# Layer 0's heads: one load for the products of four heads, and a new order of the first loads in SyncE's queue

## The chip, the core and the metric

The kernel runs on one core of a Trainium2 chip. A core has five engines, each with its own instruction stream: TensorE (PE in the profile; PEld is its weight loads), VectorE (DVE), ScalarE (ACT), GpSimd (POOL) and SyncE (SP), which only issues transfers. SyncE, ScalarE and GpSimd can each issue DMAs; the profile lists the queues as q1 (SyncE), q10 (ScalarE) and q0 (GpSimd). All of them are served by the core's 16 DMA engines. The metric is device time in microseconds (us), the median of several runs.

## The reference

Four graph layers run one after the other on x (4096 nodes, 256 features) with one adjacency matrix, each with a residual and a layernorm. The change is in layer 0, an attention layer with 8 heads of 32 channels:

```python
node_feats = (x @ W.T + b).reshape(num_nodes, num_heads, half)
logit_parent = (node_feats * a[None, :, :half]).sum(axis=-1)
logit_child = (node_feats * a[None, :, half:]).sum(axis=-1)
attn_logits = logit_parent[:, None, :] + logit_child[None, :, :]
attn_logits = jax.nn.leaky_relu(attn_logits, 0.2)
attn_logits = jnp.where(jnp.abs(adj_matrix)[..., None] != 0.0, attn_logits, 0.0)
attn_probs = jax.nn.softmax(attn_logits, axis=1)
out = jnp.einsum('ijh,jhc->ihc', attn_probs, node_feats)
...
x = _layernorm(x + _L0_gnn_ref(x, ..., adj), axis=-1)
x = _layernorm(x + _L1_gnn_ref(x, adj, L1_gnn_weight, L1_gnn_bias), axis=-1)
```

The exponential of leaky_relu(p + c) is a product of a factor of the row and a factor of the column, with one pair of factors where p + c is positive and another where it is not. So the softmax's sums split into products that don't depend on the sign, and a correction over the edges where the sign is positive.

## The kernel before, in words

**Layer 0 has two stages.** `sums0` reads x and the adjacency, computes the features, and multiplies the adjacency with the features times the factors for all heads at once. It leaves in DRAM: `nad` (the adjacency as bytes), `gmd` (the column factors times the features, in three bfloat16 parts, 396 bytes for one row and head), `lpd` (the parent logits, one row of 4096 numbers a head) and `zd` (the products that don't depend on the sign, 33 numbers a row and head). A branch follows (`choose0`, line 375): all engines read one number that says whether the factors stay in range, and otherwise run another version, `general0`.

**Then come the heads**, the loop that the change touches (lines 296 to 364). It runs over two halves of four heads, within a half over four chunks of 1024 rows (`it`), within a chunk over the half's four heads (`hh`). One pass of the inner loop, a head, goes over 32 blocks of 128 columns in 8 groups of 4 (`g`). For each group

- four comparisons of the row logits `lpb` (one row broadcast to 128 partitions, 0.52 MB) with a column's logit make `sg`: on VectorE (line 270) in groups 2, 5 and 7, on ScalarE (line 276) in the others;
- VectorE combines `sg` with the adjacency's bytes `na` into the mask `gt` (line 272 or 278);
- TensorE multiplies 32 times (line 331): the mask's 128x128 pieces with `gm`, 198 columns wide, into `acc`.

After the last group VectorE reduces `acc` (line 337), scales it (341), adds the halves (344) and `z` (345), and divides by the last column (347, 348). There are four slots for `gt`, three for `sg`, two each for `lpb` and `z`. The masks of groups 0 and 1 of the first head are made in advance, in `sums0` (`early_mask`), with their factors in `gm0` and the first head's row logits in `first`; so the first head asks for groups 2 to 7 first.

**The loads of the heads** stand in three queues. SyncE issues, for the first chunk of a half, `na` (line 301) and `gm` of the first head (303) group by group, then `gm` of the other three heads (306), and for the second half x and the rows kept of the first half (308, 310). GpSimd issues `lpb` (line 236) and `z` (316) head by head, and the store of a chunk's result (354). The next layers' weights are loaded by `add_w1` (lines 778 to 784): layer 1's weight and bias on ScalarE's queue (through `load_w`, line 115, and `load_row`, 121), three attention weights of layer 2 on GpSimd's. The call stands at the end of layer 0's code, but the tiles are free earlier, and the scheduler puts these loads near the start of the heads.

**The order of the work** in the heads is set by the framework's scheduler, from the order of the code, the free slots and what an instruction depends on; the loops of `sums0` and of layers 1 to 3 are ordered by hand. [...]

Layer 1 begins with TensorE's transposes of X (line 370) and the product with `weight1` (line 823).

Of the kernel before, what the change touches and what calls it, by code (L numbers as in the profile page):

```python
# [9 lines left out]
F32 = mybir.dt.float32  # L10
# [13 lines left out]
P = 128  # L24
# [26 lines left out]
def row_broadcast(v, n):  # L51

    return bass.AP(tensor=v.tensor, offset=v.offset, ap=[[0, P], [1, n]])


class Net:
# [159 lines left out]
    def layer0(self):  # L216
        nc, tc, NB, D, N = self.nc, self.tc, self.NB, self.D, self.N
        H, C = 8, 32
        C1 = C + 1
        IT = min(1024, N)  # L220
        Q = IT // P
        keep = self.ctx.enter_context(tc.tile_pool(name="l0k", bufs=1, space=DRAM))
        self.fits = keep.tile([1, 1], I32, name="fits")
        with ExitStack() as ctx:
            pool = ctx.enter_context(tc.tile_pool(name="l0", bufs=1))
# [6 lines left out]
            fac = pool.tile([P, 4, NB, H], F32, name="fac")  # L232
            lpd = dram.tile([H, N], F32, name="lpd")

            def row_logits(t, h, it):
                nc.gpsimd.dma_start(t, bass.AP(tensor=lpd.tensor, offset=lpd.offset + h * N + it * IT, ap=[[0, P], [1, IT]]))
                return t

            first = pool.tile([P, IT], F32, name="lpb0")
# [5 lines left out]
            zd = dram.tile([NB, P, H, C1], F32, name="zd")  # L245
# [19 lines left out]
            def mask(gt, sg, na, lpb, g, h):  # L265

                bits = [t.rearrange("p k i -> p (k i)").bitcast(U32) for t in (gt, sg, na)]
                if g % 8 in (2, 5, 7):
                    for k in range(4):
                        nc.vector.tensor_scalar(sg[:, k, :], lpb, nlc[:, 4 * g + k, h:h + 1], 2.0 ** -5,  # L270
                                                op0=ALU.is_ge, op1=ALU.mult, saturate=False)
                    nc.vector.tensor_tensor(*bits, ALU.bitwise_and)
                else:

                    for k in range(4):
                        nc.scalar.activation(sg[:, k, :], lpb, AF.Sign, scale=-1.0, bias=nlc[:, 4 * g + k, h:h + 1],  # L276
                                             saturate=False)
                    nc.vector.scalar_tensor_tensor(bits[0], bits[1], SIGN_ABOVE, bits[2],  # L278
                                                   op0=ALU.logical_shift_right, op1=ALU.bitwise_and)

            self.sums0(both, nlc, fac, lpd, nad, zd, gmd, lambda: row_logits(first, 0, 0), early_mask)
            self.choose0(fac, zd, gmd, gm0)

# [4 lines left out]
            work = ctx.enter_context(tc.tile_pool(name="l0w", bufs=2))  # L288
# [2 lines left out]
            gm = gp.tile([P, NB, H // 2, 6 * C1], BF16, name="gm")  # L291
            na = gp.tile([P, NB, IT], U8, name="na")

            later = []
            per_head = Q // 2 // (H // 2)
            for half in range(2):
                for it in range(N // IT):
                    i0 = it * Q
                    begun = 2 if it == half == 0 else 0
                    for g in [*range(begun, NB // K), *range(begun)]:  # L300
                        nc.sync.dma_start(na[:, g * K:(g + 1) * K], nad[it, :, g * K:(g + 1) * K, :])
                        if it == 0:
                            nc.sync.dma_start(gm[:, g * K:(g + 1) * K, 0], gmd[half, :, g * K:(g + 1) * K, 0])
                    for hh in range(1, H // 2 if it == 0 else 0):
                        for g in range(0, NB // K, 2):
                            nc.sync.dma_start(gm[:, g * K:(g + 2) * K, hh], gmd[half, :, g * K:(g + 2) * K, hh])
                    if half:
                        nc.sync.dma_start(X[:, i0:i0 + Q, :], xr[:, i0:i0 + Q, :])
                        y0 = work.tile([P, Q, D // 2], F32, name="y0", bufs=1)
                        nc.sync.dma_start(y0, yd[i0:i0 + Q].rearrange("b p d -> p b d"))  # L310
                    y = work.tile([P, Q, H // 2, C], F32, name="y")
                    for hh in range(H // 2):
                        h = half * (H // 2) + hh
                        lpb = row_logits(work.tile([P, IT], F32, name="lpb"), h, it) if h or it else first
                        z = work.tile([P, Q, C1], F32, name="z")
                        nc.gpsimd.dma_start(z, zd[i0:i0 + Q, :, h].rearrange("b p c -> p b c"))
                        acc = psum.tile([P, Q, 256], F32, name="acc")
                        for g in range(NB // K):

                            head0 = g < 2 and half == it == hh == 0  # L320
                            if head0:
                                gt = gt0[:, g * K:(g + 1) * K, :]
                            else:
                                gt = work.tile([P, K, IT], FP8, name="gt", bufs=4)
                                sg = work.tile([P, K, IT], FP8, name="sg", bufs=3)
                                mask(gt, sg, na[:, g * K:(g + 1) * K, :], lpb, g, h)
                            for k in range(K):
                                jc = g * K + k
                                for q in range(Q):

                                    nc.tensor.matmul(acc[:, q, :6 * C1], gt[:, k, q * P:(q + 1) * P],  # L331
                                                     gm0[:, jc, :] if head0 else gm[:, jc, hh, :],
                                                     start=(jc == 0 and q % 2 == 0),
                                                     stop=(jc == NB - 1 and q % 2 == 1))

                        red = work.tile([P, Q, 2 * C1], F32, name="red")
                        nc.vector.tensor_reduce(red, acc[:, :, :6 * C1].rearrange("p q (s c) -> p q c s", s=3),
                                                AX.X, ALU.add)

                        red = red.rearrange("p q (s c) -> p q s c", s=2)  # L340
                        nc.vector.tensor_mul(red, red, fac[:, 0:2, i0:i0 + Q, h].rearrange("p s q -> p q s").unsqueeze(3)
                                             .to_broadcast([P, Q, 2, C1]))
                        t1 = red[:, :, 0, :]
                        nc.vector.tensor_add(t1, t1, red[:, :, 1, :])
                        nc.vector.tensor_add(t1, t1, z)
                        r = work.tile([P, Q], F32, name="r")
                        nc.vector.reciprocal(r, t1[:, :, C])
                        nc.vector.tensor_mul(y[:, :, hh, :], t1[:, :, :C], r.unsqueeze(2).to_broadcast([P, Q, C]))
                        for xs in later[:per_head]:
                            self.layernorm(work, xs, xs, nc.gpsimd, bufs=6)  # L350
                        del later[:per_head]
                    y = y.rearrange("p q h c -> p q (h c)")
                    if not half:
                        nc.gpsimd.dma_start(yd[i0:i0 + Q].rearrange("b p d -> p b d"), y)
                        continue

                    if i0 + Q == NB:
                        self.add_w1()
                    engine = nc.vector if i0 + Q == NB else nc.gpsimd
                    for q in range(0, Q, 2):  # L360
                        xs = X[:, i0 + q:i0 + q + 2, :]
                        nc.gpsimd.tensor_add(xs[:, :, :D // 2], xs[:, :, :D // 2], y0[:, q:q + 2])
                        engine.tensor_add(xs[:, :, D // 2:], xs[:, :, D // 2:], y[:, q:q + 2])
                        later.append(xs)
            self.later = later
            acc = psum.tile([P, Q, 256], F32, name="acc").rearrange("p q c -> p (q c)")
            for c in range(2):
                half = acc[:, c * 512:(c + 1) * 512]
# [408 lines left out]

    def add_w1(self):
        nc, pool = self.nc, self.pool1
        self.weight1, self.bias1 = self.load_w(pool, self.w1, "w1"), self.load_row(pool, self.b1, "bias1")  # L780
        aw1, aw3, aw2, _ = self.attention_parts()
        for t, w in ((aw1, self.aw1t), (aw3, self.aw3t)):
            nc.gpsimd.dma_start(t, w.rearrange("(c p) m -> p c m", p=P))
        nc.gpsimd.dma_start(aw2, self.aw2t)

    def attention_parts(self):

# [1250 lines left out]
```

## Time and profile before

| | |
|---|---|
| median of 3 runs | 3946.61 us (3946.18 to 3950.18) |
| the profiled execution | 3947.67 us, its span 3946.0 us |
| mean granted TensorE clock | 0.994 |
| line 331 on TensorE | 577.3 to 1284.8 us |
| TensorE, VectorE, ScalarE busy from 577 to 1285 us | 701.35, 685.73, 663.92 of 708 us |
| loads of lpb; of z (32 each, GpSimd's queue) | 512 KB, 4.1 us to landing; 132 KB, 3.3 us |
| issue of one z; of one lpb on GpSimd | 0.90 us; 0.56 us |

All times are counted from the span's start. A group of instructions is shown with its line, engine, operation, the tiles that it writes and reads, how often it ran, its busy time, the mean of one, and the idle time of its engine just before it with what ended most of that. "to landing" is the time from a DMA's issue until its data is there. A wait is put down to what ended last, by inference from the semaphores. The granted clock (PEclk) is a share of TensorE's full speed.

### The profile page before, as it was taken

To read this page: it belongs to the slowest core of one execution; us is meant where nothing else is said; L and a number is where in the kernel's file an instruction comes from. 1 tells how busy PE (TensorE), PEld (TensorE's weight loads), DVE (VectorE), ACT (ScalarE), POOL (GpSimd) and SP (SyncE) were. 2 spreads that over 40 slices of the span, in tenths; PEclk is the share of its full clock that TensorE was granted. 3 is DMA by queue.
4 is the path that set the end of the run, shared out by engine and by line. 5 is a ranking of instruction groups with operands and counts; after the bars stand their busy time and mean duration, and the time that the engine had idled before them with its cause. 6 is when DMAs were issued, how large, how long until landed. Compare 5 with 4: busy or idle time off the path is not lost. (4 is left out here: it accounts for less than half of the span.)

```text
span 3946.0 us, 68781 instructions
## 1 busy us (share of the span) xinstructions
PE 3879.5 (98%) x25081; PEld 3361.6 (85%) x25081; DVE 2993.1 (76%) x6637; ACT 2742.9 (70%) x5121; POOL 1167.5 (30%) x1402
## 2 busy tenths in 40 slices
PE   8999999999999999999999999999999999999898
PEld 7999999999999887578888888866888888888686
DVE  6444449999999444667878788838999999999364
ACT  5434449999998322578888888736888888888232
POOL 1222220111444222311111111114665565555211
PEclk9999999999999999999999999999999999999999
DMA  4666667244221796533332323463333333335541
GB/s 118 204 207 203 219 196 209 82 117 120 77 92 44 281 374 254 148 113 98 98 99 93 103 94 103 156 195 102 102 107 117 105 106 105 117 107 195 199 145 45
DMA packets 317565, 557.38 MB, mean 141 GB/s; under 512 B 72806, under 2 KB 139894, under 8 KB 313110
## 3 DMA queue, kind: packets, MB, share of 16 engines
q1 hardware_dynamic: 242528, 396.99, 30.9%
q0 software_dynamic: 32224, 98.75, 7.7%
q10 hardware_dynamic: 42454, 57.04, 4.2%
q8 instruction: 203, 3.33, 0.3%
q14 instruction: 156, 1.28, 0.1%
HBM read 386.71 MB, written 165.94 MB: 140 GB/s over the span
## 5 line engine op out<-in xcount | busy, mean ns | idle before, releaser
L1411 PE MATMUL ps_a<-X,aT 128*128 128x256 f32 x4096 | 968.9, 379 | 1.3 <-ACT h L1555 1.1
L1411 PEld LDWEIGHTS ps_a<-X,aT 128*128 128x128 f32 x4096 | 773.4, 190 | 127.5 <-issue 3.9
L331 PE MATMUL acc<-gm,gt 128*128 128x198 bf16 x8192 | 701.4, 248 | 11.7 <-DVEq L375 5.3
L331 PEld LDWEIGHTS <-gt 128*128 128x128 fp8e4 x8192 | 699.5, 97 | 13.5 <-issue 7.2
L276 ACT ACTIVATE sg<-lpb,nlc 128x1024 fp8e4<-128x1024 f32 x632 | 663.9, 1135 | 43.4 <-DVE gt L278 29.3
L180 PE MATMUL ps_r<-XD,adj_piece 128*128 128x512 f32 x1888 | 528.4, 414 | 0.0
L601 PE MATMUL pz<-src,ar 128*128 128x264 f32 x4096 | 500.0, 284 | 0.4 <-DVE big L399 0.4
L601 PEld LDWEIGHTS pz<-src,ar 128*128 128x128 f32 x4096 | 499.8, 188 | 0.5 <-issue 0.5
L1138 ACT ACTIVATE ja<-e,nc 128x2048 uint8<-128x2048 f32 x240 | 480.9, 2004 | 2.0
L1404 ACT COPY aT<-ps_tp 128x512 f32<-128x512 f32 x512 | 296.4, 579 | 216.0 <-PE ps_tp L1402 208.7
L180 PEld LDWEIGHTS ps_r<-XD,adj_piece 128*128 128x128 f32 x1888 | 332.9, 189 | 68.8 <-issue 12.9
L1203 DVE MAX8 cand<-v 128x8 f32<-128x256 f32 x1024 | 347.2, 412 | 4.4
L1253 DVE SCALAR_TENSOR_TENSOR e<-e,edge 128x512 f32<-128x512 f32 x512 | 347.6, 750 | 2.1
L561 ACT ACTIVATE nb<-ar 128x512 uint8<-128x512 f32 x256 | 147.6, 623 | 279.5 <-DVE ar L558 170.8
L1402 PE MATMUL ps_tp<-ident,e 128*128 128x128 f32 x2048 | 308.0, 273 | 0.7 <-DVE e L1253 0.7
L1199 DVE SCALAR_TENSOR_TENSOR v<-e,hi 128x2048 f32<-128x2048 f32 x128 | 300.3, 2346 | 2.4
L1402 PEld LDWEIGHTS ps_tp<-ident,e 128*128 128x128 f32 x2048 | 256.8, 142 | 52.1 <-DVE e L1253 0.9
L558 DVE CAST ar<-a 128x1024 fp32r<-128x1024 f32 x128 | 88.9, 694 | 266.7 <-PE pz L601 266.6
L270 DVE TENSOR_SCALAR sg<-lpb,nlc 128x1024 fp8e4<-128x1024 f32 x384 | 285.8, 779 | 6.0 <-SPq L375 3.9
L1047 ACT ACTIVATE e<-ps_logit 128x1024 f32<-128x1024 f32 x256 | 260.2, 1027 | 26.5 <-PE ps_logit L1045 26.3
L1045 PE MATMUL ps_logit<-kT,q 128*128 128x512 f32 x1024 | 274.2, 409 | 1.4 <-ACT e L1047 1.2
L854 PE MATMUL ps_adj<-XD,adj_piece 128*128 128x512 f32 x1024 | 239.8, 394 | 0.0
(404 smaller groups left out, 5599.0 us busy)
## 6 DMA issues: line engine op xcount, KB each, us to landing
adj_piece<-adjs SPq DMA_DIRECT2D x552, 256.0 KB, 2.7
a<-in_adjt_dram SPq DMA_DIRECT2D x256, 256.0 KB, 3.1
adjs<-adj_piece SPq DMA_DIRECT2D x96, 512.0 KB, 3.1
na<-nad SPq DMA_DIRECT2D x64, 512.0 KB, 5.5
lpb<-lpd POOLq DMA_DIRECT2D x32, 512.0 KB, 4.1
nad<-nb POOLq DMA_DIRECT2D x128, 128.0 KB, 2.7
na<-nad ACTq DMA_DIRECT2D x16, 1024.0 KB, 8.8
gmd<-gb POOLq DMA_DIRECT2D x64, 198.0 KB, 2.8
```

Of the source, the lines that this page charges most:

```text
L180: nc.tensor.matmul(ps, a[:, k, :], rhs(jc).rearrange("p s d -> p (s d)"), start=(jc == 0), stop=(jc == self.NB - 1))
L270: nc.vector.tensor_scalar(sg[:, k, :], lpb, nlc[:, 4 * g + k, h:h + 1], 2.0 ** -5, op0=ALU.is_ge, op1=ALU.mult, saturate=False)
L276: nc.scalar.activation(sg[:, k, :], lpb, AF.Sign, scale=-1.0, bias=nlc[:, 4 * g + k, h:h + 1], saturate=False)
L331: nc.tensor.matmul(acc[:, q, :6 * C1], gt[:, k, q * P:(q + 1) * P], gm0[:, jc, :] if head0 else gm[:, jc, hh, :], start=(jc == 0 and q % 2 ...
L601: nc.tensor.matmul(pz[q][:, t, :W], ar[:, q, k, :], src[:, jc, t, s], start=(jc == 0 and s == 0), stop=(jc == NB - 1 and s == 1))
L1138: nc.scalar.activation(ja, e[:, s * HALF:(s + 1) * HALF], f, bias=nc1, accum_out=fs[:, i + s:i + s + 1])
L1199: nc.vector.scalar_tensor_tensor(v, ec, hi, ec, op0=ALU.is_lt, op1=ALU.mult, accum_out=sb[:, s:s + 1])
L1203: nc.vector.max(cand[:, 8 * j:8 * j + 8], v[:, k * 256:(k + 1) * 256])
L1253: nc.vector.scalar_tensor_tensor(ec, ec, edge[:, j:j + 1], ec, op0=ALU.is_ge, op1=ALU.mult)
L1402: nc.tensor.transpose(pt[:, k * P:(k + 1) * P], e[:, jc * P:(jc + 1) * P], self.ident)
L1404: nc.scalar.copy(aT, pt)
L1411: nc.tensor.matmul(pa[:, :D], aT[:, k * P:(k + 1) * P], X[:, jc, :], start=(jc == 0), stop=(jc == NB - 1))
```

## The change

The products `z` of a half's four heads are read in one load for each chunk, with one slot (so each element run is 528 bytes and not 132). In the very first chunk this load and head 1's row logits are issued by SyncE, behind the loads of group 4; in the other chunks GpSimd issues z, ahead of the chunk's row logits in the code. `first` and `second` serve heads 0 and 1 of the first chunk. `add_w1` issues all five loads on SyncE's queue; as built they stand behind the four loads of x and ahead of the second chunk's bytes.

```diff
-            def row_logits(t, h, it):
-                nc.gpsimd.dma_start(t, bass.AP(...))
+            def row_logits(t, h, it, queue=nc.gpsimd):
+                queue.dma_start(t, bass.AP(...))
                 return t
...
+            def products_of(i0, half, queue):
+                z = work.tile([P, Q, H // 2, C1], F32, name="z", bufs=1)
+                queue.dma_start(z, zd[i0:i0 + Q, :, half * H // 2:(half + 1) * H // 2].rearrange("b p h c -> p b h c"))
+                return z
...
                         if it == 0:
                             nc.sync.dma_start(gm[:, g * K:(g + 1) * K, 0], gmd[half, :, g * K:(g + 1) * K, 0])
+                        if begun and g == 4:
+                            z = products_of(i0, half, nc.sync)
+                            second = row_logits(work.tile([P, IT], F32, name="lpb"), 1, 0, nc.sync)
+                    if not begun:
+                        z = products_of(i0, half, nc.gpsimd)
...
-                        lpb = row_logits(work.tile([P, IT], F32, name="lpb"), h, it) if h or it else first
-                        z = work.tile([P, Q, C1], F32, name="z")
-                        nc.gpsimd.dma_start(z, zd[i0:i0 + Q, :, h].rearrange("b p c -> p b c"))
+                        lpb = (first, second)[h] if it == 0 and h < 2 else \
+                            row_logits(work.tile([P, IT], F32, name="lpb"), h, it)
...
-                        nc.vector.tensor_add(t1, t1, z)
+                        nc.vector.tensor_add(t1, t1, z[:, :, hh, :])
...
     def add_w1(self):
         nc, pool = self.nc, self.pool1
-        self.weight1, self.bias1 = self.load_w(pool, self.w1, "w1"), self.load_row(pool, self.b1, "bias1")
+        self.weight1 = pool.tile([P, 2, self.D], F32, name="w1")
+        nc.sync.dma_start(self.weight1, self.w1.rearrange("(c p) m -> p c m", p=P))
+        self.bias1 = pool.tile([P, self.D], F32, name="bias1")
+        nc.sync.dma_start(self.bias1, row_broadcast(self.b1, self.D))
         aw1, aw3, aw2, _ = self.attention_parts()
         for t, w in ((aw1, self.aw1t), (aw3, self.aw3t)):
-            nc.gpsimd.dma_start(t, w.rearrange("(c p) m -> p c m", p=P))
-        nc.gpsimd.dma_start(aw2, self.aw2t)
+            nc.sync.dma_start(t, w.rearrange("(c p) m -> p c m", p=P))
+        nc.sync.dma_start(aw2, self.aw2t)
```

More of the change, by code (lines that the diff above doesn't have):

```diff
@@ L233, in layer0 @@
             lpd = dram.tile([H, N], F32, name="lpd")
-            def row_logits(t, h, it):
-                nc.gpsimd.dma_start(t, bass.AP(tensor=lpd.tensor, offset=lpd.offset + h * N + it * IT, ap=[[0, P], [1, IT]]))
+            def row_logits(t, h, it, queue=nc.gpsimd):
+                queue.dma_start(t, bass.AP(tensor=lpd.tensor, offset=lpd.offset + h * N + it * IT, ap=[[0, P], [1, IT]]))
                 return t
```

## The prediction

> **What bounds the kernel now.** I read the page first, then TensorE's waits around the change, the timeline where they fall, the clock in short stretches there, and the DMA queues. From the page:
>
> ```profile
> PE 3879.5 (98%) x25081; PEld 3361.6 (85%) x25081; DVE 2993.1 (76%) x6637; ACT 2742.9 (70%) x5121; POOL 1167.5 (30%) x1402
> ...
> L331 PE MATMUL acc<-gm,gt 128*128 128x198 bf16 x8192 | 701.4, 248 | 11.7 <-DVEq L375 5.3
> ```
>
> TensorE is the bound, and in the stage that is changed (line 331) it idles 11.7 us in all, so no reordering of loads can win more than that and what a stall costs in clock. TensorE's waits from 570 to 1330 us (what, us in total, times, longest):
>
> ```profile
> PE acc L331 <- DVEq L375: 5.3, 1, 5.3
> PE acc L331 <- DMA gm<-gmd: 3.4, 1, 3.4
> PE acc L331 <- DVE gt L278: 2.8, 2, 1.7
> ```
>
> The first is the branch ahead of the heads, which the change leaves alone. The last two fall at 1138.03 and 1227.37, where GpSimd's layernorms run beside VectorE; no load is late there. The 3.4 us are what the change can reach. The timeline (start, duration, engine, line):
>
> ```profile
> 578.81 1.09 SPq L301 DMA_DIRECT2D na<-nad  x1
> 579.08 0.62 POOL L236 DMA_DIRECT2D lpb<-lpd  x1
> ...
> 582.65 1.23 DVE L272 TENSOR_TENSOR gt<-sg,na 128x1024 uint32<-128x1024 uint32 x1 [1.45 <-DMA na<-nad]
> ...
> 587.40 1.23 DVE L278 SCALAR_TENSOR_TENSOR gt<-sg,na 128x1024 uint32<-128x1024 uint32 x1 [2.07 <-DMA na<-nad]
> ...
> 590.42 15.76 PE L331 MATMUL acc<-gm,gt 128*128 128x198 bf16 x164 [3.39 <-DMA gm<-gmd]
> ...
> 591.89 1.23 DVE L278 SCALAR_TENSOR_TENSOR gt<-sg,na 128x1024 uint32<-128x1024 uint32 x1 [1.94 <-DMA na<-nad]
> ```
>
> VectorE waits for the bytes of groups 2, 3 and 4 in turn; group 3's were issued at 578.81 and landed at 587.40, its factors (gm) issued at 580.06 landed at 590.42, where TensorE had run dry at 587.03. Clock after the stall (second figure from the right-hand group, PEclk; then DMA share, GB/s):
>
> ```profile
> 588.00:590.00 2.00, 0.00 (x0) 0.10 (x1) 1.96 (x3) 1.34 (x2) 0.00 (x0) 1.00 1.09 313
> 590.00:592.00 2.00, 1.58 (x10) 1.45 (x10) 0.11 (x1) 2.00 (x3) 0.00 (x0) 0.62 1.10 351
> 592.00:594.00 2.00, 2.00 (x15) 1.83 (x13) 1.97 (x3) 0.93 (x1) 0.00 (x0) 0.53 1.08 357
> 594.00:596.00 2.00, 2.00 (x27) 2.00 (x25) 2.00 (x3) 0.27 (x1) 0.00 (x0) 1.00 1.08 370
> ```
>
> The clock falls to 0.62 and 0.53 for 4 us: 2 x 0.38 + 2 x 0.47 = 1.7 us lost on top of the 3.4. Head 0 ends at 606.4 (its reduction on VectorE starts at 606.47): the five groups from 590.42 took 16.0 us. A head takes 21.76 us where nothing is late (the distance of VectorE's waits for TensorE at 908.26, 930.02 and 951.78), a group an eighth, 2.72; five are 13.6. So 2.4 us went, 1.7 of them by the clock. The DMA engines are full (1.08). Whose packets they move from 582 to 587 us (packets, MB, share):
>
> ```profile
> q0 software_dynamic: 278, 0.95, 64.4%
> q1 hardware_dynamic: 370, 0.61, 39.2%
> ```
>
> GpSimd's queue (q0: sums and row logits for later) takes more than SyncE's (q1), which has what is needed next.
>
> [...] q0's packets average 0.95 MB / 278 = 3.4 KB, a gm row of SyncE's is 396 bytes, and the share is 64 to 39. [...]
>
> **The change, part by part.**
>
> *Loads at the start.* Before, ahead of or beside group 3 to 5's loads stand w1 (0.26 MB), two z (0.27), two row logits (1.05) and three attention weights (0.14): 1.72 MB in other queues. After, GpSimd sends one load, head 2's row logits (0.52); SyncE's queue is na2, gm2, na3, gm3, na4, gm4, z of four heads (0.54), head 1's row logits (0.52), na5 ... A group is 0.52 + 0.20 MB. I count bytes against what moved before in each 5 us from 577: 0.99, 1.56, 1.66, 1.82, 1.69 MB, that is 0.99 by 582, 2.55 by 587, 4.21 by 592, 6.03 by 597, 7.72 by 602. A landing comes later: na5 (2.70 MB of q1, which had moved 2.46 by 592 and did 0.364 a us) is out at 592.7 and landed at 593.85; I take 1.1 us.
> - Group 3: through gm3, 1.45 + 0.52 = 1.97 MB: out at 582 + 0.98/0.31 = 585.1, landed 586.2; its bytes 0.6 us sooner. Its mask is done by 586.8 (1.14 us from start to start of the next). TensorE is through group 2 at 587.03: no wait, and no half clock. Gain 3.4 + 2.4 = 5.8 us.
> - Group 4: bytes through 2.50 MB, landed 588.0, mask 589.1, needed 589.75. No wait.
> - Group 5: z and row logits now stand before it: 4.29 MB, out at 592.2, landed 593.3 to 593.5, mask 594.6; needed 592.47. A new stall of 2.1 us. It is under the 3.4 that halved the clock, and the stall of 1.72 at 1227 left the clock at 1.00, so I add nothing for it.
> - Groups 6 and 7: 5.0 and 5.7 MB, landed 595.4 and 597.3, masks 596.7 and 598.4, needed 597.3 and 600.0: none.
> - Head 1's first factors (L306): 7.81 MB, out at 602.3, landed 603.4; head 0 ends at 594.6 + 3 x 2.72 = 602.8: another 0.6 us.
>
> Head 1 starts at 603.4 and not 606.4: 5.8 - 2.1 - 0.6, about 3.0 us. The 603.4 is a floor by itself, since these factors are the last of 7.81 MB, whichever came first.
>
> *VectorE's order.* The built order differs in head 0 alone: its reduction (1.72 us) now stands before head 1's masks 1 and 2, not behind them. It starts at 602.8, so mask 1 is done at 602.8 + 1.72 + 1.14 = 605.7, needed 603.4 + 2.72 = 606.1. Hidden with 0.4 us to spare; without that, up to 0.5 us. Later masks: ScalarE (four activations of 1.05 us a group) starts head 1 when group 5's slot is free, 594.6 against 595.73 before, and has groups 0, 1, 3, 4 at 598.8, 603.0, 607.2, 611.4; VectorE's mask 4 is at 612.6, three comparisons (0.69) and mask 5 at 615.8, needed 603.4 + 5 x 2.72 = 617.0. Hidden, 1.2 us to spare.
>
> *ScalarE.* Two issues (0.40 and 0.35 us) leave its queue; it starts masks 0.4 us sooner. Nothing: it next waits for a slot of sg (2.19 us at 588.66).
>
> *GpSimd.* 32 z issues of 0.90 us become 7, with the three weights and one logits load gone: 30 fewer. GpSimd is off the path. With one z slot, the next z waits for the last head's sum; behind it on the queue are the store of y and a row of logits needed a head later (21.8 us). Free; a lost cover would show as ScalarE waiting for lpb. Whether fewer issues speed VectorE beside them is bounded by its rows: at 1253.70 an sg takes 1.06 us beside a z, at 702.30 it takes 0.70. At most 24 x 0.36 = 9 us of VectorE's time, at least nothing; its two stalls fall beside layernorms, not z, so I take nothing, up to 1 us.
>
> *Weights behind X.* Five DMAs (0.5 MB, 1.5 us at 338 GB/s) stand ahead of chunk 1's bytes in SyncE's queue from about 629 us; those wait for VectorE anyway (72 us at the longest). First use is at 1287. Nothing.
>
> *Does the gain last?* VectorE waits for TensorE eight times between 755 and 1017 us (4.5 us in all), so it follows TensorE's shift; the stalls at 1138 and 1227 arise after that and stay. Later the chain ends on TensorE.
>
> Sum: -3.0 us. The profiled execution took 3947.67 (span 3946.0 and 1.67 around it), so 3944.7; the median of the three runs is 1.06 lower, 3946.61, so **3943.6**.
>
> **Rivals.**
> 1. *The whole gain*: group 5 and head 1's factors in time, -5.8 us, 3940.8. For: SyncE's packets alone on the engines did 364 GB/s (592 to 597). Against: 4.29 MB through na5 are nearly as much as before (4.43), and the factors would have to land 2.7 us sooner than worked out.
> 2. *No gain*: the stall moves to group 5 whole, or VectorE's new order and thin lead give it back; 3946.6. For: VectorE is 97 to 99% busy in the heads. Against: its waits for TensorE.
> 3. *Slower*: z and logits in front of na5 on one queue. z's 528-byte packets may go at 248 GB/s (what the queue did with gm alone at 612 to 616). If na5 lands after 595.3, its stall passes 3.4 us, halves the clock (1.7 us) and uses up the gain; at 597.3 that is +2, 3948.6.
> 4. *The change does nothing*: logits on GpSimd's queue still crowd SyncE's; group 3 stays late. Against: 0.52 MB for 1.46. Counted with 2.
>
> **Numbers.** Forecast (-1.5 to -4.5) 0.64; whole gain 0.12; none 0.17; slower 0.07. 3940.0 to 3948.0 holds all but the slow tail; the likeliest alone is 3942.0 to 3945.2. 0.2% (7.9 us) is about what a measurement of this kernel can tell from no change: faster than that would need more than all the idling that the loads cause (0.03), slower would need na5 at about 603 (0.02), same 0.95.
>
> **What would show it.** Right: TensorE's wait at group 3 gone and its clock 1.00 after 580 us; a wait of about 2 us at group 5, with VectorE waiting for na; head 0's reduction at 602 to 604; the idling of line 331 (another number in the new file) at 10 to 11 us. Wrong: a clock under 0.7 near 595, or a wait at group 3 still; new waits in head 1; a stall for lpb.

## The result, and the profile after

The changed kernel takes 3941.09 us (median of 22 runs) where the kernel before takes 3946.96 (22 runs beside it): a ratio of 0.9985, with a 95% interval from 0.9979 to 0.9991. That is 5.9 us less (3.6 to 8.3), twice the 3.0 that were forecast. The profiled execution took 3941.38 us, span 3939.7 (before 3947.67 and 3946.0): 6.3 us less.

In the heads the page shows, of the changed kernel:

```profile
PE 3876.2 (98%) x25081; PEld 3358.8 (85%) x25081; DVE 2995.0 (76%) x6637; ACT 2741.3 (70%) x5121; POOL 1138.4 (29%) x1373
...
L340 PE MATMUL acc<-gm,gt 128*128 128x198 bf16 x8192 | 700.4, 248 | 11.7 <-DVEq L384 5.3
```

Line 340 is the old line 331. Its idle time is 11.7 us, as before: no microsecond of waiting has gone. What is 1.0 us less is the busy time, 700.4 for 701.4. TensorE's waits from 570 to 1330 us (what, us in total, times, longest) show that it has been dealt out anew:

```profile
PE acc L340 <- DVEq L384: 5.3, 1, 5.3
PE acc L340 <- DMA gm<-gmd: 2.6, 2, 1.3
PE acc L340 <- DVE gt L278: 2.4, 2, 1.7
PE acc L340 <- DVE gt L272: 1.4, 1, 1.4
```

One wait of 3.4 us for factors has become two of 1.3, and a wait for a mask (line 272) of 1.4 is new. The timeline of TensorE and VectorE places them (start, duration, engine, line; in brackets the idle time before and what ended it):

```profile
587.02 8.48 PE L340 MATMUL acc<-gm,gt 128*128 128x198 bf16 x96 [1.32 <-DMA gm<-gmd]
...
595.66 1.23 DVE L272 TENSOR_TENSOR gt<-sg,na 128x1024 uint32<-128x1024 uint32 x1 [1.00 <-DMA na<-nad]
...
596.95 8.33 PE L340 MATMUL acc<-gm,gt 128*128 128x198 bf16 x96 [1.44 <-DVE gt L272]
...
606.58 5.63 PE L340 MATMUL acc<-gm,gt 128*128 128x198 bf16 x64 [1.30 <-DMA gm<-gmd]
```

They fall at group 2, at group 5 (VectorE waits for na, now behind z and the row logits) and at head 1. Behind none of them does the clock fall (PEclk is the third figure from the right). Where the kernel before was at 0.62 and 0.53 it is 1.00, and it stays there behind the wait at group 5 and to the end of the heads:

```profile
590.00:592.00 2.00, 2.00 (x25) 2.00 (x25) 1.81 (x3) 2.00 (x3) 0.00 (x0) 1.00 1.22 327
592.00:594.00 2.00, 2.00 (x27) 2.00 (x25) 2.00 (x4) 2.00 (x3) 0.00 (x0) 1.00 1.02 395
...
597.00:602.00 5.00, 5.00 (x60) 5.00 (x61) 2.75 (x3) 5.00 (x5) 0.00 (x0) 1.00 1.08 354
```

The queues have changed places from 582 to 587 us (packets, MB, share of the engines): SyncE's q1 has twice the share of GpSimd's q0, where before it had less.

```profile
q1 hardware_dynamic: 816, 0.90, 62.6%
q0 software_dynamic: 144, 0.52, 30.0%
```

The forecast set packet sizes beside the shares (3.4 KB on GpSimd's queue, 396 bytes for a row of gm). The 144 packets of GpSimd's queue here are as large, at 3.6 KB, and have the smaller share, 30.0% where it was 64.4% before; one load was left there, 512 KB of row logits. Whether the size matters apart from what is queued, no run here separates.

From its first to its last start, line 340 takes 706.5 us (578.2 to 1284.7) where line 331 took 707.5. So the heads account for about one of the 6.3 us in this pair of executions, and it is clock and not waiting. An estimate from the windows: the half clock behind group 3's stall, worth 1.7 us before, is gone, but behind the branch the clock was low for longer (0.50 on average from 577 to 582 us, 0.68 before), which, counted from TensorE's first matmul, takes about 0.6 us back. Most of the rest is at the other end. The last store is issued at 3936.69 before and at 3934.81 after, and the span ends 9.3 us behind it before, but only 4.9 after. What lies there is on no page's list of costly groups. It is in the rows that the trace puts on the line that closes the program (`with tile.TileContext`), here first of before and then of after; the columns are the number, the durations (least, median, longest, in ns), and the first and last start:

```profile
L2034 POOLq DRAIN  x3: 40/113/9528, 3935.6 to 3945.7; - x3
```

```profile
L2046 POOLq DRAIN  x3: 40/113/5117, 3933.7 to 3939.4; - x3
```

GpSimd's part of the last layernorm is its last work. Its first closing DRAIN is recorded from there on (from 3935.6 and 3933.7, beside the last 0.6 us of that work), 9.53 us long before and 5.12 after. The last store lands 1.7 us after its issue in the kernel before, and in the changed kernel SyncE's wait for it ends 1.8 us after the issue, both well before the DRAIN's end, and the span ends 0.9 us after the DRAIN in both. That is 4.4 us of the gain.

### The profile page after: what moved, and what is told of

The parts are those of the page before. It is cut to its first block, busy times and chain, and to the rows that moved or that the text cites. A ratio compares the mean times of both kernels' runs of the same rounds, so it can differ in the third digit from the quotient of the medians.

```text
span 3939.7 us, 68711 instructions
## 1 busy us (share of the span) xinstructions
PE 3876.2 (98%) x25081; PEld 3358.8 (85%) x25081; DVE 2995.0 (76%) x6637; ACT 2741.3 (70%) x5121; POOL 1138.4 (29%) x1373
## 5 line engine op out<-in xcount | busy, mean ns | idle before, releaser
L340 PE MATMUL acc<-gm,gt 128*128 128x198 bf16 x8192 | 700.4, 248 | 11.7 <-DVEq L384 5.3
```

## The experiments

The theories, by the letters used in what was expected: A, the gain comes from the loads of the first head; B, it comes from GpSimd's DRAIN, which follows the number of its DMAs; C, the length of the DRAIN is chance; D, it depends on something else than that number. Later came E, heads and DRAIN simply add up; F and G, the DRAIN depends on the place in GpSimd's instruction stream, or on its DMAs; H, the merged load of z is what matters. In the tables, "heads" is the time from the first to the last start of the matmuls into `acc`, and it and the DRAIN are read from one profiled execution; the ratio is to the kernel before on the same chip.

**1. The changed kernel again, and each part alone.** Four kernels on one chip, beside 49 runs of before (3947.31 us).

> The changed kernel once more, unaltered. Theory A (the gain is the first head's loads, as forecast): the heads' stage (first matmul to last) is 2 to 3 us shorter than the 707.5 of before, and GpSimd's closing DRAIN is whatever it is. Theory B (the gain is GpSimd's closing DRAIN, which was 9.53 us before and 5.12 after and follows how many DMAs GpSimd has issued): the drain is 5.1 us again, the stage 706 to 707.5. Theory C (the drain's length is chance): it is a different value, anywhere from 4 to 10. Time in all: 5 to 7 us under the kernel before.

The weights alone:

```diff
# before, with add_w1 as in the change
-            nc.gpsimd.dma_start(t, w.rearrange("(c p) m -> p c m", p=P))
-        nc.gpsimd.dma_start(aw2, self.aw2t)
+            nc.sync.dma_start(t, w.rearrange("(c p) m -> p c m", p=P))
+        nc.sync.dma_start(aw2, self.aw2t)
# and the same for w1 and bias1
```

> The kernel before with only the five weight loads moved to SyncE's queue behind x: 3 DMAs fewer on GpSimd (512 for 515). Theory A: 0.40 MB less ahead of group 3, its factors about 1.2 us sooner, 1 to 2 us faster. Theory B, if the drain follows the count in a straight line (29 fewer took 4.41 us, 0.15 each): drain 9.1 us, 0.5 us faster. Theory C: any drain.

The merged load alone, on GpSimd's queue in every chunk:

```diff
+                    z = products_of(i0, half, nc.gpsimd)
...
-                        z = work.tile([P, Q, C1], F32, name="z")
-                        nc.gpsimd.dma_start(z, zd[i0:i0 + Q, :, h].rearrange("b p c -> p b c"))
```

> The kernel before with only z merged: one load of four heads a chunk, all on GpSimd, one slot; the first row logits and the weights as before; 24 DMAs fewer on GpSimd (491). Theory A: group 3 no sooner (0.54 MB of z ahead in place of 0.27), 0 to 1 us slower. Theory B: drain 5.9 us, 3.7 us faster. Theory C: any drain.

The first loads alone, z as a load a head:

```diff
+                        if begun and g == 4:
+                            zs = []
+                            for h in range(2):
+                                zs.append(work.tile([P, Q, C1], F32, name="z"))
+                                nc.sync.dma_start(zs[h], zd[i0:i0 + Q, :, h].rearrange("b p c -> p b c"))
+                            second = row_logits(work.tile([P, IT], F32, name="lpb"), 1, 0, nc.sync)
```

> The kernel before with only the first two z and head 1's row logits issued by SyncE behind group 4; z one load a head, weights as before; 3 DMAs fewer on GpSimd (512). Theory A: group 3's wait gone or under 1.5 us and the clock at 1.00, 2 to 3 us faster. Theory B: drain 9.1 us, 0.5 us faster from it. Theory C: any drain.

| | median (runs) | ratio [95%] | heads | waits for gm | DRAIN | GpSimd's DMAs |
|---|---|---|---|---|---|---|
| before | 3947.31 (49) | | 707.5 | 3.4 | 9.53 | 515 |
| changed, again | 3941.21 (21) | 0.9987 [0.9980, 0.9994] | 706.0 | 1.6 | 5.12 | 486 |
| weights alone | 3948.88 (13) | 1.0004 [0.9996, 1.0012] | 707.8 | 3.0 | 7.73 | 512 |
| merged z alone | 3948.98 (13) | 1.0003 [0.9995, 1.0011] | 707.4 | 3.0 | 6.67 | 491 |
| first loads alone | 3949.27 (13) | 1.0003 [0.9995, 1.0012] | 709.9 | 4.6 | 7.73 | 512 |

Three things follow. The DRAIN came out at 5118 ns after 5117, so it is no chance: C falls. The heads, 706.0, are 1.5 us below the 707.5 of before, less than the 2 to 3 of A. No part alone is faster, though A expected 1 to 3 us of two of them. And the first loads alone show what the forecast feared as its third rival. TensorE's timeline there, and the clock after the stall:

```profile
580.11 10.35 PE L340 MATMUL acc<-gm,gt 128*128 128x198 bf16 x96 [5.33 <-DVEq L384]
590.69 5.60 PE L340 MATMUL acc<-gm,gt 128*128 128x198 bf16 x64 [0.23 <-DMA gm<-gmd]
600.62 11.60 PE L340 MATMUL acc<-gm,gt 128*128 128x198 bf16 x115 [4.33 <-DMA gm<-gmd]
```

```profile
602.00:604.00 2.00, 2.00 (x14) 1.83 (x13) 1.23 (x1) 2.00 (x3) 0.00 (x0) 0.50 1.09 353
```

Group 3 is in time but for 0.23 us (32 matmuls a group: 96 and 64 are groups 0 to 4). But group 5's bytes stand behind z and the row logits in SyncE's queue, and the other queues still moved data of their own (from 582 to 587 us 0.25 MB on ScalarE's and 0.14 on GpSimd's; in the changed kernel none and 0.52). TensorE's wait at group 5 is 4.33 us, in the changed kernel 1.44, and the clock falls to 0.50 behind it: the heads take about 2 us more than before.

Of the DRAIN, the number of DMAs seemed to rank the four lengths (486, 491, 512, 515), which B says, though not by its straight line, which gave 5.9 us for the merged z and 9.1 for the other two. But the parts alone, with DRAINs 1.8 to 2.9 us shorter than before's, were not faster at all; so the next runs change the DRAIN and nothing in the heads.

**2. The DRAIN moved by itself.** All edits are in `sums0`, where GpSimd does little but issue stores (in the kernel before 96.8 us for nad, 35.8 for gmd, under 4 us for all else); the heads are the changed ones.

Each store of nad cut in two (614 DMAs):

```diff
-                    nc.gpsimd.dma_start(nad[it, :, g * G:(g + 1) * G, i:i + 2 * P], nb.rearrange("p g q i -> p (g q i)"))
+                    for k in range(0, G, G // 2):
+                        nc.gpsimd.dma_start(nad[it, :, g * G + k:g * G + k + G // 2, i:i + 2 * P],
+                                            nb[:, k:k + G // 2].rearrange("p g q i -> p g (q i)"))
```

> The changed kernel with one edit in sums0: each of GpSimd's 128 stores of nad is cut in two, so that GpSimd issues 614 DMAs in the program and not 486; the heads, their loads and all later work are the same. Theory B (GpSimd's closing DRAIN follows its number of DMAs and ends the program): the DRAIN is longer than the 9.53 us of the kernel before (515 DMAs), at 10 to 40 us, the end comes later by that, and the median is 3946 us or more while the heads' first to last matmul stays at 706 +- 1 us. Theory A (the gain comes from the first loads of the heads): DRAIN or not, the median stays at 3941 +- 1.5. Theory D (the DRAIN follows what else differs between these programs, not the count): the DRAIN stays at 5.1 us.

The two stores of gmd made one (454):

```diff
-                for half in range(2):
-                    nc.gpsimd.dma_start(gmd[half, :, b], gb[:, half * H // 2:(half + 1) * H // 2].rearrange("p h s c -> p h (s c)"))
+                nc.gpsimd.dma_start(gmd[:, :, b].rearrange("t p h c -> p t (h c)"), gb.rearrange("p (t h) s c -> p t (h s c)", t=2))
```

> The changed kernel with one edit in sums0: the two stores of gmd of a block (one for each half of the heads) are one store of the same bytes, so GpSimd issues 454 DMAs and not 486. Theory B: the DRAIN is shorter than 5.12 us (2 to 4.5 us), the end comes as much sooner, median 3938 to 3940.5. Theory A: the heads' stage is the same, median 3941 +- 1.5. Theory D: DRAIN 5.1 us.

Both kinds of stores on ScalarE's queue (294):

```diff
-                    nc.gpsimd.dma_start(gmd[half, :, b], ...)
+                    nc.scalar.dma_start(gmd[half, :, b], ...)
...
-                    nc.gpsimd.dma_start(nad[it, :, g * G:(g + 1) * G, i:i + 2 * P], ...)
+                    nc.scalar.dma_start(nad[it, :, g * G:(g + 1) * G, i:i + 2 * P], ...)
```

> The changed kernel with sums0's 128 stores of nad and 64 of gmd issued by ScalarE and not by GpSimd: GpSimd issues 294 DMAs. ScalarE is busy 41% of sums0, and 192 issues of 0.35 to 0.4 us are 67 to 77 us of its 577. Theory B: the DRAIN is shorter than with 454 DMAs, at most 3 us, and the end comes 2 to 4 us sooner than in the changed kernel: 3937 to 3939.5, if the first matmul of the heads still falls at 578 to 579 us. Theory A: 3941 +- 1.5, or more where ScalarE's issues are late. Theory D: DRAIN 5.1 us.

And the kernel before once more, unaltered:

> The kernel before, unaltered (515 DMAs of GpSimd). Theory B and theory D: its closing DRAIN is 9.53 us again, within 0.02 us. If the length were chance, anything from 5 to 10 us.

| | median (runs) | ratio [95%] | heads | DRAIN | median less DRAIN |
|---|---|---|---|---|---|
| before (40 runs on this chip) | 3947.88 | | 708.6 | 9.53 | 3938.4 |
| nad cut | 3940.23 (20) | 0.9981 [0.9974, 0.9987] | 706.7 | 4.06 | 3936.2 |
| gmd joined | 3943.05 (13) | 0.9990 [0.9981, 0.9998] | 706.1 | 6.83 | 3936.2 |
| stores on ScalarE | 3944.10 (13) | 0.9992 [0.9984, 1.0000] | 705.8 | 7.89 | 3936.2 |

The row of nad cut, with the most DMAs of these, has the shortest DRAIN, and that of ScalarE's stores, with the fewest of all, the second longest:

```profile
L2048 POOLq DRAIN  x3: 40/113/4055, 3935.1 to 3939.8; - x3
...
L2046 POOLq DRAIN  x3: 40/113/7893, 3936.8 to 3945.3; - x3
```

So the ranking by number was an accident of four points, and my expectation was wrong in sign for three programs of three: most DMAs gave the shortest DRAIN, the fewest the longest of these. Before's came out at 9528 ns, to the nanosecond. But the other half of B stands: the medians follow the DRAIN. Less its own DRAIN, each of the three is at 3936.2, and the changed kernel at 3941.21 - 5.12 = 3936.1 (on another chip, where before was 0.6 us lower), with DRAINs from 4.06 to 7.89 us. A alone would have all of them at 3941, within 1.5 us; nad cut is within it, the other two are not. That the four agree to 0.1 us is in part luck, since the intervals of these medians reach about 3 us to either side.

**3. Before with another DRAIN, two parts, and a test of what the DRAIN follows.** Four kernels on one chip, beside 33 runs of before (3946.86). First the kernel before with nad's stores cut in two, by the edit shown above.

> The kernel before with the 128 stores of nad of sums0 each cut in two; the heads and their loads are those of before. So far the medians less the closing DRAIN were 3936.0 to 3936.2 us in four programs with the changed heads (changed kernel, nad cut, gmd joined, stores on ScalarE) and 3938.0 in the kernel before. Theory E (DRAIN and heads add up; the heads gave some 2 us, the DRAIN some 4.4): whatever DRAIN this program shows, its median is 3938 us plus that DRAIN, within 1.5 us; with a DRAIN of 4 to 6 us that is 3942 to 3944, so a gain with no change of the heads. Theory A (the DRAIN is of no account, the heads gave all): the median stays at 3947 to 3948.

Then the changed kernel with instructions on GpSimd that are no DMAs:

```diff
+            junk = wp.tile([P, 1], F32, name="junk")
...
+                    if n % 4 == 0 and n < 4 * 29:
+                        nc.gpsimd.memset(junk, 0.0)
```

> The changed kernel with 29 more instructions on GpSimd in sums0, each a memset of a column of 128 numbers that nobody reads: as many instructions as the kernel before has on GpSimd, and 486 DMAs still. Theory F (the DRAIN depends on where in GpSimd's instruction stream the program ends): the DRAIN is not 5.12 us, and if this is all, near the 9.53 of before; the median is then 3936.1 plus the DRAIN, up to 3945.7. Theory G (the DRAIN depends on the DMAs that GpSimd issued): 5.12 us within 0.02, median 3941.2 +- 1.

Two of the three parts, weights and first loads, by the edits of the first set put together:

> The kernel before with two of the three parts: the next layers' five weight loads on SyncE's queue, and the first two products z and head 1's row logits on SyncE's queue behind group 4; the products of later heads stay one load a head on GpSimd's queue. Theory A for the heads: the wait for group 3's factors goes (under 1 us) only where all other queues are cleared ahead of it, which these two parts do and either alone didn't; waits for gm of 2 to 3 us in all as in the changed kernel, first to last matmul 706 to 707 us. Theory H (the merged load of z is what matters): the wait at group 3 stays at 3 us or more and the clock falls after it. The median is 3936 to 3938 plus this program's DRAIN.

And another order, in the changed kernel with nad's stores cut:

```diff
-                        if begun and g == 4:
-                            z = products_of(i0, half, nc.sync)
+                        if begun and g == 5:
                             second = row_logits(work.tile([P, IT], F32, name="lpb"), 1, 0, nc.sync)
...
                             nc.sync.dma_start(gm[:, g * K:(g + 2) * K, hh], gmd[half, :, g * K:(g + 2) * K, hh])
+                            if begun and hh == 1 and g == 0:
+                                z = products_of(i0, half, nc.sync)
+                        if begun and hh == 1:
+                            third = row_logits(work.tile([P, IT], F32, name="lpb"), 2, 0, nc.sync)
```

> The changed kernel with nad's stores cut in two, and another order of the first loads in SyncE's queue: head 1's row logits behind group 5 (not 4), the products z behind the first factors of head 1, and head 2's row logits, which GpSimd issued at the start, behind all factors of head 1. Theory A for the heads: the waits of TensorE for group 2's factors (1.3 us), for group 5's mask (1.4) and for head 1's factors (1.3) shrink to 1.5 us in all, so first to last matmul 703.5 to 705 us, and the median is 3933.5 to 3935 plus the DRAIN. Rival: VectorE or the floor of the bytes sets head 1's start, the waits move to later groups and the stage stays at 706 +- 0.7; median 3936 plus the DRAIN.

| | median (runs) | ratio [95%] | heads | DRAIN | median less DRAIN |
|---|---|---|---|---|---|
| before | 3946.86 (33) | | not taken here | 9.53 | 3937.3 |
| before, nad cut | 3943.52 (13) | 0.9995 [0.9987, 1.0004] | 708.1 | 5.28 | 3938.2 |
| changed, 29 memsets | 3937.55 (10) | 0.9973 [0.9964, 0.9983] | 706.2 | 5.12 | 3932.4 |
| weights and first loads | 3944.11 (12) | 0.9992 [0.9983, 1.0000] | 707.9 | 5.93 | 3938.2 |
| later z | 3937.06 (8) | 0.9975 [0.9965, 0.9986] | 703.6 | 4.06 | 3933.0 |

*Before, nad cut.* The heads keep their wait (3.1 us for gm) and their 708.1 us, the DRAIN is 5.28, and the median is 3.3 us lower (2.0 by the ratio), where the DRAINs differ by 4.25; less its own, it is at 3938.2, and 3938 was expected. The interval of this ratio alone still holds no change (up to 1.0004), so this run doesn't decide by itself; together with the four programs above it fits E better than A.

*Memsets.* With 29 instructions more and the same 486 DMAs the DRAIN is 5.12 again:

```profile
L2049 POOLq DRAIN  x3: 40/112/5118, 3931.1 to 3936.8; - x3
```

So 29 instructions more don't move it, and F falls; every edit that did move it changed GpSimd's DMAs. (The median is another matter: G had it at 3941.2 within 1 us, and it is 3.7 below.) What in the DMAs sets it is open. It isn't their number alone (614 gave 4.06 us, 643 gave 5.28, 486 gave 5.12, 294 gave 7.89) or their bytes alone, since weights alone took 144 KB off GpSimd's queue and first loads alone 776 KB, and both had 7732 ns. Yet there is an order in part: with three DMAs fewer than before's 515, by either part, and with six fewer, by both, the DRAIN falls from 9.53 in two equal steps of 1.80 us. Here are weights alone, first loads alone, and the two together:

```profile
L2037 POOLq DRAIN  x3: 44/113/7732, 3938.0 to 3946.3; - x3
L2043 POOLq DRAIN  x3: 44/113/7732, 3943.4 to 3951.7; - x3
L2046 POOLq DRAIN  x3: 40/113/5933, 3938.1 to 3944.6; - x3
```

The same step would take the merged z, with 24 fewer, far below its 6.67 us.

*Weights and first loads.* The wait at group 3 is gone, as A expected, and the clock stays at 1.00. But TensorE waits at group 5, then for a mask and at head 1:

```profile
579.34 15.61 PE L340 MATMUL acc<-gm,gt 128*128 128x198 bf16 x160 [5.32 <-DVEq L384]
597.43 2.89 PE L340 MATMUL acc<-gm,gt 128*128 128x198 bf16 x32 [2.48 <-DVE gt L272]
600.86 5.61 PE L340 MATMUL acc<-gm,gt 128*128 128x198 bf16 x64 [0.54 <-DVE gt L278]
607.79 4.43 PE L340 MATMUL acc<-gm,gt 128*128 128x198 bf16 x50 [1.31 <-DMA gm<-gmd]
```

The heads take 707.9 us, no better than before, where 706 to 707 was expected. The merged z isn't needed to clear group 3's wait (H falls), though this pair of parts won nothing by clearing it.

*Later z.* TensorE runs head 0 without a stop (256 matmuls) and then waits for head 1's factors:

```profile
578.73 23.98 PE L343 MATMUL acc<-gm,gt 128*128 128x198 bf16 x256 [5.50 <-DVEq L387]
603.89 8.28 PE L343 MATMUL acc<-gm,gt 128*128 128x198 bf16 x95 [1.19 <-DMA gm<-gmd]
```

The heads take 703.6 us, and the median is 9.8 us under before (5.5 to 13.8 by the interval), the lowest of all these kernels, though the memsets' 3937.55 is within the scatter of it. Less its DRAIN it is at 3933.0, 3.2 below nad cut's 3936.2, which has the changed order and the same DRAIN; 703.5 to 705 and 3933.5 to 3935 had been expected.

**What stays open.** First, the parts alone: less their DRAINs they are at 3941.2 (weights), 3942.3 (merged z) and 3941.5 (first loads), 3.4 to 4.5 us above before's 3937.8 on that chip, and their heads explain it for none but the first loads (2 us of 3.7). The intervals of these ratios are 3 us to either side, so part of it may be scatter, but the merged z's 4.5 us isn't explained by that alone. The profiles don't hold the missing time: the merged z's profiled execution took 3944.51 us, 4.5 below its own median, and less the DRAIN it is at before's 3937.8. From the heads' last matmul to the DRAIN, in code that no edit touches, the fourteen profiled executions took 2646.4 to 2653.3 us, so single executions differ there by more than any effect in the heads. The sum of heads and DRAIN (E) thus holds for the programs with the changed heads but the memsets', and for two of the five with others; it is not shown as a general rule. Secondly, the 29 memsets made the kernel faster by more than the heads and the DRAIN give; that is told at the end. Thirdly, that the DRAIN could be hidden by giving the last layernorms' two GpSimd instructions to VectorE, so that it would start before the last blocks are done, wasn't tried. In the changed kernel it could give about 2.2 us, an estimate: SyncE's wait for the last store ends at 3936.6 us and the DRAIN at 3938.84.

## Why the prediction was right, and where its sum was not

The forecast of 3943.6 lay in the right direction, its range (3940.0 to 3948.0) holds the 3941.09, and the change is within 0.2%. But the sum was right for a reason that was not all of it: 3.0 us from the heads, against 1.9 from the heads and 4.4 from the end. The gain lies outside the 1.5 to 4.5 us of its main case, and the median below the 3942.0 to 3945.2 that it called likeliest. With the DRAIN of before it would have been at about 3945.5 (3941.09 + 4.41), an estimate. Nothing in the forecast could tell whether the DRAIN would grow or shrink, so that it added to the gain and did not hide it is luck.

- *Group 3: no wait, no half clock.* Right. The wait is gone, and the clock is 1.00 from 584 to 600 us, where the kernel before showed 0.62 and 0.53 (0.50 again in its second profile).
- *Group 5: a new stall of 2.1 us, below the 3.4 behind which the clock had fallen.* Right in place and cause (VectorE waiting for na) and in the clock (1.00 behind it), 1.44 us in size, since everything came later: TensorE ran dry at 595.50 us and not at 592.47, and the mask was there at 596.95 and not at 594.6.
- *Head 1's factors: 0.6 us.* 1.30 us measured. They were to land at 603.4; TensorE, dry at 605.28 and not at 602.8, started on them at 606.58.
- *Groups 2 and 4: no wait.* Wrong for group 2, which lost 1.32 us. The step that failed is the landing times, which were all counted from the start of the kernel before's transfers. There SyncE's first load was issued at 577.90, 0.6 us after TensorE's first matmul of the heads; in the changed kernel at 579.71, 1.5 us after it. So by 582 us 0.34 MB had moved, not 0.99. The waits for factors differ between executions, too: the changed kernel's second profile shows 1.6 us in two waits, the longer of them 1.2, where the first shows 2.6.
- *The gain of the heads, 3.0 us.* Three profiles with the heads of before (one with nad's stores cut) give 707.5, 708.6 and 708.1 us from first to last matmul, mean 708.1; the changed kernel and the programs with the same heads give 706.5, 706.0, 706.7, 706.1, 705.8 and 706.2, mean 706.2. That is 1.9 us. The medians less the DRAINs say the same, the memsets' apart: 3936.2 against 3937.3 to 3938.4. The difference from 3.0 is in the terms above: in the first profile 1.32 + 1.44 + 1.30 = 4.1 us of new waits for 2.7 in the sum. They eat up the wait that went, and what is left is about what the half clock had cost, 1.7 us by the forecast's own reading.
- *GpSimd: 30 fewer issues are off the path and worth nothing, up to 1 us.* (29 by the profiles, 515 and 486.) This is the step that failed most. It asked which engine waits for GpSimd in the heads, and nothing there does. But it did not ask what else depends on what GpSimd issued. Its closing DRAIN, 4.06 to 9.53 us long in programs that differ in GpSimd's DMAs, is recorded from the last layernorm on and ends 0.9 us before the span does: 9.53 - 5.12 = 4.4 us. The page before the change gave it only as a share of 0%, and its 9.3 us from the last store to the end were never split up.
- *VectorE's order, ScalarE's issues, the weights behind x: nothing.* No new wait in the heads comes from them: behind head 1's start the waits are the two for line 278 that were there before (2.4 us, before 2.8), and layer 1 starts with the same two waits of 0.7 us.
- *The rivals.* "The whole gain", 3940.8, is next to the measured time and yet not what happened: the heads did not gain 5.8. "Slower" did not happen, but what it describes did in another program: in the first loads alone TensorE waited 4.33 us at group 5, the clock fell to 0.50, and the heads took 709.9 us for 707.5.

Of the clock the forecast had two readings, 0.53 behind a wait of 3.39 us and 1.00 behind one of 1.72, and took 3.4 us as the length that a stall has to pass. The profiles show the clock fall behind shorter ones: 2.86 us (merged z alone) were followed by 0.53, and waits of 3.04 to 3.10 (weights alone, before with nad cut, and before again) by 0.50. The longest wait for factors or a mask that left it at 1.00 was 2.48 us (weights and first loads). First the merged z alone, then the two parts:

```profile
589.63 4.53 PE L335 MATMUL acc<-gm,gt 128*128 128x198 bf16 x32 [2.86 <-DMA gm<-gmd]
590.00:592.00 2.00, 2.00 (x16) 1.84 (x14) 0.00 (x0) 0.00 (x0) 0.00 (x0) 0.53 1.12 341
```

```profile
598.00:600.00 2.00, 2.00 (x27) 2.00 (x25) 0.42 (x1) 2.00 (x3) 0.00 (x0) 1.00 1.08 358
```

## What to carry to other kernels

Account for the end of the span as for any stage: take the time from the last useful store to the end, and name the row that fills it, since a closing DRAIN of 4 to 10 us on GpSimd stands in no list of busy groups and moved here with DMAs that were issued milliseconds before. When a change alters a queue's DMAs, compare medians after taking such a fixed term off, or its few microseconds pass for the effect under study. And a load moved out of the way is moved in front of something else: it paid here to order loads by when their data is used (z behind head 1's factors, later row logits last), which gave the heads 4.5 us (one profile) where the first order gave 1.9 (six).

## What was not expected of the hardware

GpSimd's DRAIN was the same to 2 ns for one and the same program (9528 and 9528 ns; 5117, 5118, and 5118 with memsets added), and it was anything from 4.06 to 9.53 us between programs that differ in GpSimd's DMAs, with no order by their number that holds for all of them.

Twenty-nine memsets of 128 numbers that nobody reads, and a tile of 4 bytes a partition for them, made the program about 3 us faster, with the same heads and the same DRAIN: it is 9.3 us below the kernel before on its chip, the changed kernel 5.9 and 6.1. The profiles place it in `sums0`, in the matmuls into pz, here of the changed kernel and of that with memsets (busy us and mean ns of one):

```profile
L610 PE MATMUL pz<-src,ar 128*128 128x264 f32 x4096 | 500.8, 285 | 0.4 <-DVE big L408 0.4
```

```profile
L613 PE MATMUL pz<-src,ar 128*128 128x264 f32 x4096 | 497.6, 284 | 0.4 <-DVE big L408 0.4
```

TensorE idles 0.4 us for them in both, its clock is 1.00 from 170 us on, and a matmul takes 0.8 ns less in the mean, 3.2 us in all. In the other thirteen profiles these matmuls took 500.0 to 501.3 us, so 497.6 isn't scatter. It is one build of one program. Whether the tile's shift of what lies behind it in memory or the memsets themselves do that was not tried. It is larger than the effect of the change in the heads, and a warning for every comparison of a few microseconds.
